# K's seventh block product by quarter products, and three moves around it, in two attention layers on one Trainium2 core

## The chip, the core and the metric

The kernel runs on one core of a Trainium2 chip. Five engines work side by side and meet at semaphores: TensorE (PE in the profile; its weight loads are PEld), VectorE (DVE), ScalarE (ACT), GpSimd (POOL) and SyncE (SP), which issues the DMA transfers. Only TensorE multiplies matrices, and it writes to PSUM; VectorE and ScalarE read PSUM, GpSimd reads only SBUF. Each engine takes its instructions in the order in which the program wrote them. The metric is the device time of one execution in microseconds (us). All arithmetic is in float32.

## What is computed

Two layers of the same form follow one another over x of shape (8, 512, 32, 32): 8 images, 512 channels, 1024 pixels (tokens). Per layer and image:

```python
xn = group_norm(x)                               # layer 0: 8 groups, scale and bias; layer 1: 32 groups
qkv = einsum('oc,bcn->bon', qkv_w, xn) + qkv_b   # 1536 x 512 weights
q, k, v = split(qkv)                             # 8 heads of 64 channels
attn = softmax(einsum('bhdi,bhdj->bhij', q, k) / sqrt(64))
out = einsum('bhij,bhdj->bhdi', attn, v)
x = einsum('oc,bcn->bon', proj_w, out) + proj_b + x
```

## The kernel before

**Units.** One layer of one image is a unit; units 0 to 7 are layer 0, units 8 to 15 are layer 1. Each unit has two stages. In the projection stage TensorE forms Q, K and V of the unit (unit 0: Q, V, K) and then the output projection of the unit before (`project`). In the attention stage it goes through 8 chunks (4 head pairs by 2 halves of the query tokens) of 8 steps: scores (L809), exponential on ScalarE (L817), products with V (L837), row sums on VectorE (L854, L856).

**Block products.** A projection multiplies 512 x 512 weights by 512 x 1024 activations. `blocks` splits both into two by two blocks and needs seven block products instead of eight, at the price of additions. They are numbered 1 to 7 and come in the order 1, 6, 2, 7, 5, 4, 3. The factors are sums and differences of blocks: `mix_weights` makes those of the weights, `mix_right` those of the activations (`t1`, `t2`, `t4`, and in place `b12 = b22 - b12`, the right factor of product 7). Products 1, 2 and 3 accumulate in PSUM over others: `bx`, `by` and `bz` are two banks each (apair[0], sbank[0], apair[1]), and after each product VectorE or ScalarE takes what is finished (`c11`, `summed`, `others`) before a later product writes there. A plain block product (`block_product`, L413) is four matmuls of 128 partitions by 512 columns in Q, K and the projection, eight of 256 columns in V.

**Inner products.** For the block products listed in `INNER` a second level of the same scheme is used in all units but 0 (`inner_products`, L452): the 256 x 256 by 256 x 512 product becomes seven matmuls of 128 x 128 by 256 columns. Their left factors lie ready in DRAM (`mix_inner_left` made them once per layer in three 128 x 128 tiles per block product; `load_inner_left` fetches them for each unit). Their right factors are four subtractions of 128x256 per block product (`mix_inner`), by GpSimd for Q's and by VectorE for K's first (room: K's output tile 3, not yet written). Four of the seven results are not added by TensorE. ScalarE copies them from PSUM to a tile of four quarters (L457) as soon as they stand, since the next of them is accumulated on top of the last (1, then 6, then 7, in the region `one`; 5 in the region `two`). GpSimd adds them later: two folds (L467, L468) and then adds into q, k or the result (`rests`, L635 to L638 and L734).

**What sets the order of the work.** It is written by hand. `rest` maps a number g to a list of small steps; `projections` calls the steps of g when it has passed the g-th of 21 marks, seven in each of its three projections (`done`). `attention` returns the steps that the next unit's projections carry for this unit: `parts`. Mark 3 has the last head pair's reciprocals, mark 10 its division and its bias (`divide_last`: L919 on VectorE, two L926 on ScalarE), 15 the load of the projection's left factors, 17 to 20 the projection's right factors (mixing and `mix_o`, the latter on GpSimd for unit 6, B - 2). A step recorded at a mark stands in its engine's queue at that place. Steps called from the marks show in the profile under L566, whatever they do.

**Norm of the next unit.** While a unit is in attention, `at_step` runs the next unit's group norm: statistics (L277), aggregation (L281), group means and variances by small matmuls with a group matrix (L289), scale and shift (L315 to L327), application on ScalarE (L331) and the first two right factors (L179). In unit 0 all but the statistics come one chunk later than in other units (`late`). At the very start `norm_first` norms unit 0's input in two halves, with idle matmuls between the small ones (L358), which multiply x's first tile with itself; nothing reads their result.

**Rooms.** Tiles come from pools with a fixed number of buffers; a tile's first writer waits until the readers of the one before in that buffer are done. Here: `o1`, `o2`, `o4` of `tpool` (room for Q's copies, then the projection's factors), `p` (4), `acc` (2), `tr` (2, among them u2 of Q, K, V and the projection, and the projection's left factors) and `rb` (1: the last pair's reciprocals, then the projection's u3).

Of the kernel before, what the change touches and what calls it, by code (L numbers as in the profile page):

```python
# [11 lines left out]
F32 = mybir.dt.float32  # L12
# [6 lines left out]
P = 128  # L19
# [13 lines left out]
def fast_path(ctx, tc, x, qkv_wT, proj_wT, vecs, groups, out, flag):  # L33
# [15 lines left out]
    nc = tc.nc  # L49
    B, C, N = x.shape  # L50
    CC = C // P
    D = C // HEADS
    NT = N // P
# [4 lines left out]
    BL = 32  # L58
    SCALE = 1.0 / math.sqrt(D)

    INNER = {"q": (2, 5, 4, 3), "k": (1, 2, 5, 4, 3), "o": (2, 3, 4)}
    assert D == H and C == FD

    def pool(name, bufs, **kw):
# [135 lines left out]
        s1, s2, s4 = made  # L200
        return {1: a11, 2: a12, 3: s4, 4: a22, 5: s1, 6: s2, 7: a21}

    def mix_inner_o(u, right, k, engine):


        sub = engine.tensor_sub
        b = right[k]
        b11, b12 = b[:, 0, :FD2], b[:, 0, FD2:]
        b21, b22 = b[:, 1, :FD2], b[:, 1, FD2:]
        tag = {2: "x2", 3: "x1", 4: "x4"}[k]  # L210
        t = tpool.tile([P, 4, FD2], F32, tag=tag, name=f"ro{k}_{u}")
        t1, t2, t4 = (t[:, i, :] for i in range(3))
        sub(t1, b12, b11)
        sub(t2, b22, t1)
        sub(b12, b22, b12)
        sub(t4, b21, t2)
        return {1: b11, 2: b21, 3: b22, 4: t4, 5: t1, 6: t2, 7: b12}, t[:, 3, :]

    def mix_inner_left(l, lefts):

# [124 lines left out]
    def norm_first(xs, weights, mixing):  # L345

        bank = sbank[1][:, 0, :]  # L350
        (
            (first, stats_1, aggregate_1, means_1, variances_1, scales_1, apply_1, apply_now_1),
            (second, stats_2, aggregate_2, means_2, variances_2, scales_2, apply_2, apply_now_2),
        ) = (norm_parts(0, xs, lo, lo + 2) for lo in (0, 2))

        def idle_products(n):
            for _ in range(n):
                nc.tensor.matmul(  # L358
                    sbank[0][:, 0, : 2 * P], xs[:, 0, :P], xs[:, 0, : 2 * P], start=True, stop=True
                )  # L360

        idle_products(3)
        for h in range(NH):
            stats_1(0, h)
        mixing_w = weights(first["last"])
        for h in range(NH):
            stats_1(1, h)
        aggregate_1()
        stats_2(2, 0)
        means_1(bank)  # L370
        idle_products(3)
        stats_2(2, 1)
        variances_1(bank)
        idle_products(4)
        for h in range(NH):
            stats_2(3, h)
        aggregate_2()
        scales_1()
        apply_now_1(0, 0)
        apply_1(1, 0)  # L380
        apply_now_1(0, 1)
        apply_1(1, 1)
        means_2(bank, first["last"])
        idle_products(3)
        mixing_w[0]()

        def rest():
            variances_2(bank)
            mixing[0]()
            scales_2()  # L390
            for h in (1, 0):
                apply_now_2(2, h)
                apply_2(3, h)
            mixing[1]()
            mixing_w[1]()

        return rest, mixing_w
# [19 lines left out]
                )  # L417

    def blocks(name, left, right, tokens, c11, others, done, u3_in, summed, inner={}, rests=None,
               between=None, behind=None, p1=None):  # L420

# [10 lines left out]
        def inner_products(bank, k, first=False):  # L434
# [25 lines left out]
                step(j)  # L460
            return (rest, partial(step, order[-1])) if k == 1 else rest

        def add_rest(r, h, rest, alone=None):

            if rest is not None:
                add = nc.gpsimd.tensor_add
                add(rest[:, 0, FD2:], rest[:, 0, FD2:], rest[:, 1, FD2:])  # L467
                add(rest[:, 1, FD2:], rest[:, 1, :FD2], rest[:, 1, FD2:])  # L468
                rests(r, h, rest, alone)

        def work(pool, tag, k):
# [18 lines left out]
        else:  # L490
# [4 lines left out]
            nc.scalar.copy(p1, bx)  # L495
            done(sums)
            products(by, 6, True, False)
        u2 = work(trpool, "tr", "u2")
        summed(0, u2, by, p1)
        done(sums)  # L500
        rest = inner_products(bx, 2, fresh)
        c11(bx, p1 if fresh else None, rest)
        add_rest(0, 0, rest)
        done(sums)
        products(by, 7, False, False)
        u3 = work(*u3_in, "u3")
        summed(1, u3, by, p1)
        done(sums)
        twice = inner_products(bz, 5, True)
        others(1, 1, bz, u3, twice)  # L510
        add_rest(1, 1, twice, u3)
        done(sums)
        rest = inner_products(by, 4)
        others(1, 0, by, p1)
        add_rest(1, 0, rest)
        done(sums)
        rest = inner_products(bz, 3)
        others(0, 1, bz, u2, twice)
# [14 lines left out]
    def inner_of(w, sel, left):  # L533


        x, z, s1 = apair[0], apair[1], sbank[1]
        p = room_of(ppool, "p")
        plan = {
            "q": {
                2: (s1, z, ORDER, room_of(tpool, "o1")), 5: (s1, x, ORDER, room_of(tpool, "o2")),  # L540
                4: (x, s1, ORDER, room_of(tpool, "o4")), 3: (s1, x, ORDER, room_of(tpool, "o1")),
            },
            "k": {
                1: (s1, z, ORDER_1, lambda _: w.k[1].rearrange("p (a b) -> p a b", a=2)),
                2: (s1, z, ORDER, room_of(tmppool, "tmp")),
                5: (s1, x, ORDER_5, p), 4: (x, s1, ORDER, p), 3: (s1, x, ORDER, p),
            },
        }[sel]
        return {
            k: (inner_lefts(k, left[k], w.made[sel][k]), w.inner[k], *plan[k]) for k in INNER[sel]  # L550
        }

    def projections(w, rest, between=None):
# [94 lines left out]
        def values():  # L648
            w.v = vpool.tile([P, NT, C], F32, tag="v", name=f"v_{u}")

            def of_tokens(t):
                return t.rearrange("p a (b o) -> p (a b) o", b=2)

            def v11(bank, more, _):
                to, cols = w.v[:, : NT // 2, :FD2], of_tokens(bank)
                w.last["v"].append(
                    nc.scalar.copy(to, cols) if more is None else
                    nc.vector.tensor_add(to, cols, of_tokens(more))
                )

            def v_others(r, h, bank, more, _=None):
                w.last["v"].append(
                    nc.vector.tensor_add(
                        w.v[:, ts(h, NT // 2), ts(r, FD2)], of_tokens(bank), of_tokens(more)
                    )
                )

            blocks(
                f"v_{u}", w.lefts[2], w.right, True, v11, v_others, done, (ppool, "p"), plain_sum,
                **early["v"],  # L670
            )

# [101 lines left out]
    def attention(w, at_step, at_end):  # L774
# [185 lines left out]
        transposed(n_chunks - 1)  # L960
        reduced(n_chunks - 1)

        def divide_last():
            divide(CC - 1)
            for h in range(NH):
                add_bias(CC - 1, h)

        w.right_o, mixing = mix_right(f"o_{u}", *w.ao)
        w.inner_o = None
        parts = {3: [lambda: reciprocals(CC - 1)], 10: [divide_last], 17: mixing[:2], 18: mixing[2:3],  # L970
                 19: mixing[3:]}
        if u in (0, B):
            return parts

# [12 lines left out]
        def mix_o(k):  # L987

            engine = nc.gpsimd if u == B - 2 else nc.vector
            right, room = mix_inner_o(u, w.right_o, k, engine)  # L990
            if k == INNER["o"][-1]:
                lefts.append(room[:, :P])
                nc.sync.dma_start(lefts[-1], src[:, len(lefts) - 1, :])
            w.inner_o[k] = right

        def finish():
            for i, k in enumerate(INNER["o"]):
                w.inner_o[k] = (inner_lefts(k, w.left[k], lefts[3 * i : 3 * i + 3]), w.inner_o[k])

        parts[15] = [load_left]  # L1000
        parts[18] += [partial(mix_o, 2)]
        parts[19] += [partial(mix_o, 3)]
        parts[20] = [partial(mix_o, 4)]
        w.finish = finish
        return parts

# [26 lines left out]
    for u in range(2 * B):  # L1033
# [10 lines left out]
        if u > 0:  # L1044
            w.made, w.inner, parts = old.made_next, {}, {}
            for k in INNER["q"]:
                room = ppool.tile([P, 4, FD2], F32, tag="p", name=f"r{k}_{u}")
                w.inner[k], parts[k] = mix_inner(right[k], room, nc.gpsimd)

            room = w.k[3].rearrange("p (a b) -> p a b", a=4)  # L1050
            w.inner[1], parts[1] = mix_inner(right[1], room, nc.vector)
            for part in parts[2] + parts[5]:
                part()  # L1053
            for g, k in ((2, 4), (3, 3), (5, 1)):
                rest.setdefault(g, []).extend(parts[k])
        if u == B + 1:
            rest.setdefault(16, []).extend(mixing_o)
# [11 lines left out]
        if u == 0:  # L1069
            def first_left_part(i, part):  # L1070
# [1 line left out]


            after = [14] * len(INNER["q"]) + [
                14 + {1: 1, 2: 3, 5: 5, 4: 6, 3: 7}[k] for k in INNER["k"]
            ]
            for i, part in enumerate(mix_inner_left(0, dict(zip("qk", lefts)))):
                rest.setdefault(after[i], []).append(partial(first_left_part, i, part))
# [59 lines left out]
            if old.u == B - 1:  # L1138
                (left_o,), mixing_o = mix_weights(1, [load_proj(1, "wproj")], nc.vector, 3)


        late = 1 if u == 0 else 0

        def at_step(s, state):
            if nxt is None:
                return
            st, stats, aggregate, means, variances, scales, apply, _ = nxt
            c, t = divmod(s, NT)

            if left_parts and t in (3, 7) and s >= (3 + late) * NT - 1:  # L1150
                left_parts.pop(0)(state["exp"][-1])

            pair = (c + 1) % 2
            free = state["free"][pair]
            c -= late
            if u == 0 and NT // 2 <= s < NT:
                stats_of(2 * s - NT, 2 * s - NT + 1)
            if c == 1 and t == 1:
                aggregate()
# [27 lines left out]
        nc.vector.tensor_reduce(low[:, 1:2], okay, AX.X, ALU.min)  # L1187
        nc.vector.tensor_mul(both, low[:, 0:1], low[:, 1:2])

    project_last(old, [part for g in (3, 10) for part in rest[g]] + [verdict])  # L1190
    nc.tensor.matmul(turns[0][:1, :1], both, ones[:, :1], start=True, stop=True)
    nc.scalar.copy(flag, turns[0][:1, :1])

# [262 lines left out]
```

## Time and profile before

| | |
|---|---|
| median of 4 runs | 3269.28 us (3268.52 to 3269.92) |
| profiled execution | 3269.09 us, span 3267.3 us, TensorE clock 1.00 |
| busy in the span | PE 3253.4, DVE 2612.5, ACT 1623.9, POOL 1092.5 us |
| one inner unit's projection stage, unit 2 | 404.61 to 496.27 us, PE busy 91.66 of 91.66 |
| the same stage, others | DVE 63.62, ACT 26.39, POOL 59.64 us busy |
| one attention stage, unit 1 | 294.35 to 404.61 us, PE busy 110.26 of 110.26 |

The profile is of one execution. A row of the timeline is an instruction, or several alike in a row: start in us from the span's start, length, engine, line of the program, operation, tile written and tiles read, shape, count, and in brackets the idle time of that engine before it with what ended it. float32 matmuls leave two records each; their ends are modelled, so distances between starts tell more than lengths. In the list of waits the columns are: who waited for whom, us in total, times, longest.

### The profile page before, as it was taken

The page shows a single profiled execution, that of the slowest core. Times are in us where ns is not written, and L with a number is a line of the kernel's source. Part 1 is how long each engine was busy: PE and PEld are TensorE (multiplying, and loading weights), DVE is VectorE, ACT ScalarE, POOL GpSimd, SP SyncE. Part 2 cuts the span into 40 slices and gives each one's busy share as a digit, 9 for nine tenths or more (in the row PEclk, how much of TensorE's full clock was granted, in tenths as well). Part 3 has the DMA queues.
Part 4 walks back from the last instruction along what each step waited for, and adds up shares of the span by engine and source line. Part 5 has one row for each costly group of instructions (what it writes and reads, how often), then busy time and mean ns, then how long its engine had stood idle before and what let it go on. Part 6 is the DMA issues. An engine that isn't in the chain of part 4 may idle for free.

```text
span 3267.3 us, 56136 instructions
## 1 busy us (share of the span) xinstructions
PE 3253.4 (100%) x22080; PEld 1839.8 (56%) x22080; DVE 2612.5 (80%) x3364; ACT 1623.9 (50%) x2212; POOL 1092.5 (33%) x1125
## 2 busy tenths in 40 slices
PE   9999999999999999999999999999999999999999
PEld 5455474654746547465574645646556474564743
DVE  5886968879687896878968779687896978969777
ACT  1652726536274462744627436373563735637354
POOL 2051161531616216066160603506125061340610
PEclk9999999999999999999999999999999999999999
DMA  2112120121201212023120111201212012120221
GB/s 94 41 43 78 40 83 28 49 79 43 79 28 43 79 44 85 22 69 114 48 85 29 56 61 55 85 15 42 86 43 85 15 45 83 43 85 15 67 74 48
DMA packets 78395, 188.54 MB, mean 58 GB/s; under 512 B 22064, under 2 KB 27056, under 8 KB 78128
## 3 DMA queue, kind: packets, MB, share of 16 engines
q1 hardware_dynamic: 78128, 184.88, 16.4%
q8 instruction: 179, 2.93, 0.4%
q14 instruction: 88, 0.72, 0.1%
HBM read 144.47 MB, written 38.80 MB: 56 GB/s over the span
## 4 chain that ended last, share of the span: by engine, by line
PE 99%; DVE 0%; DMA 0%; ACT 0%; issue 0%; SPq 0%; DVEq 0%; ACTq 0%
PE a L837 27%; PE s L809 26%; PE s L413 16%; PE a L413 13%; PE a L452 9%; PE s L452 7%; PE a L809 1%; PE s L755 0%; PE a L755 0%; DMA xn<-x_dram 0%; PE s L358 0%; DVE stats L277 0%; PE a L289 0%; ACT p L817 0%; DVE u_q L612 0%
## 5 line engine op out<-in xcount | busy, mean ns | idle before, releaser
L817 ACT ACTIVATE p<-s 128x1024 f32<-128x1024 f32 x976 | 998.3, 1024 | 597.5 <-PE s L809 567.2
L837 PE MATMUL a<-p,v 64*64 64x512 f32 x8192 | 1099.7, 589 | 0.2 <-ACT p L817 0.2
L809 PE MATMUL s<-q,k 64*64 64x512 f32 x7808 | 1058.1, 590 | 0.0
L856 DVE TENSOR_TENSOR acc<-acc,p 128x1024 f32<-128x1024 f32 x768 | 964.2, 1255 | 75.5 <-ACT p L817 22.1
L837 PEld LDWEIGHTS a<-p,v 64*64 64x64 f32 x8192 | 382.7, 131 | 496.7 <-ACT p L817 350.9
L809 PEld LDWEIGHTS s<-q,k 64*64 64x64 f32 x7808 | 383.4, 133 | 432.8 <-issue 426.0
L1053 POOL TENSOR_TENSOR r<-xn 128x256 f32<-128x256 f32 x30 | 52.3, 1743 | 1135.6 <-DVE acc L856 807.2
L854 DVE TENSOR_TENSOR acc<-p,p 128x1024 f32<-128x1024 f32 x128 | 156.4, 1222 | 17.5 <-ACT p L817 17.5
L309 POOL TENSOR_TENSOR y<-var,half 128x4 f32<-128x4 f32 (+1 forms) x17 | 33.1, 1949 | 401.1 <-DVE var L307 401.1
L638 POOL TENSOR_TENSOR k<-k,m_k 128x512 f32<-128x512 f32 x120 | 165.8, 1397 | 0.0
L869 DVE STREAM_TRANSPOSE tr<-acc 128x1024 f32<-128x1024 f32 x128 | 158.0, 1234 | 0.0
L879 DVE TENSOR_REDUCE red<-tr 128x32 f32<-128x1024 f32 x128 | 153.9, 1202 | 0.6
L638 POOL TENSOR_TENSOR q<-q,m_q 128x512 f32<-128x512 f32 x120 | 153.1, 1290 | 0.0
L863 DVE TENSOR_TENSOR ao<-a,tmp 128x512 f32<-128x512 f32 x128 | 88.0, 687 | 66.7 <-ACT tmp L862 66.7
L467 POOL TENSOR_TENSOR m_o<-m_o 128x256 f32<-128x256 f32 x39 | 28.7, 736 | 332.9 <-ACT m_o L457 332.9
L495 ACT COPY p_o<-a 128x1024 f32<-128x1024 f32 x15 | 15.2, 1012 | 244.1 <-PE a L413 244.1
L526 DVE TENSOR_TENSOR u_v<-s,p_v 128x1024 f32<-128x1024 f32 x32 | 39.2, 1224 | 121.2 <-POOL k L635 96.2
L457 ACT COPY m_q<-s 128x256 f32<-128x256 f32 x150 | 55.9, 373 | 146.7 <-PE s L452 132.6
L413 PE MATMUL s<-x_t,s2w 128*128 128x512 f32 x256 | 117.5, 592 | 0.0
L413 PE MATMUL s<-xn,w 128*128 128x512 f32 x256 | 115.5, 594 | 1.8 <-DVE xn L179 1.8
L413 PE MATMUL a<-w,xn 128*128 128x256 f32 x496 | 112.1, 379 | 0.0
L926 ACT ACTIVATE ao<-ao,vec 128x512 f32<-128x512 f32 x128 | 88.4, 714 | 43.0 <-DVE ao L919 43.0
(296 smaller groups left out, 4884.1 us busy)
## 6 DMA issues: line engine op xcount, KB each, us to landing
rb<-drec SPq DMA_DIRECT2D x128, 256.0 KB, 3.9
xn<-mid SPq DMA_DIRECT2D x36, 512.0 KB, 7.7
xn<-x_dram SPq DMA_DIRECT2D x32, 512.0 KB, 7.0
x<-x_dram SPq DMA_DIRECT2D x32, 512.0 KB, 4.8
il<-ilk SPq DMA_DIRECT2D x15, 960.0 KB, 6.3
x<-mid SPq DMA_DIRECT2D x28, 512.0 KB, 4.6
il<-ilq SPq DMA_DIRECT2D x15, 768.0 KB, 4.3
mid<-u_o SPq DMA_DIRECT2D x32, 256.0 KB, 2.0
```

The lines of the kernel that those rows point to most:

```text
L413: nc.tensor.matmul(dst, at[:, c, ts(i, P)], moving[:, c, :], start=start and c == 0 and not (tokens and i % 2), stop=stop and c == 1, skip ...
L452: nc.tensor.matmul(dst[j], a[j], b[j], start=j in (1, 5) or first and j in (2, 4), stop=j not in (1, 6), skip_group_check=True,)
L638: w.last[sel].append(add(cols, cols, rest[:, i, :]))
L809: nc.tensor.matmul(bank[e * H : (e + 1) * H, j, :], w.k[pr][j * H : (j + 1) * H, t * P + e * H : t * P + (e + 1) * H], w.q[pr][j * H : (j ...
L817: exp = nc.scalar.activation(p, bank, AF.Exp, scale=SCALE)
L837: nc.tensor.matmul(banks[r][j * H : (j + 1) * H, :], w.v[rows, t, lo : lo + D], p[rows, j, :], start=(t == 0), stop=(t == NT - 1),)
L854: nc.vector.tensor_add(acc, state["first"], p)
L856: nc.vector.tensor_add(acc, acc, p)
L863: i1 = nc.vector.tensor_add(w.ao[pr // 2][:, pr % 2, ts(qh, FD)], banks[1], tmp)
L869: nc.vector.transpose(tr, state["acc"].pop(c))
L879: nc.vector.tensor_reduce(red[:, :, qh, :], state["tr"].rearrange("p j (f i) -> p j f i", i=BL), AX.X, ALU.add)
L926: nc.scalar.activation(cols, cols, AF.Identity, bias=vec[:, units[u][0], VB, pr : pr + 1])
```

## The change

It has four parts.

1. K's product 7 joins the inner products (`INNER["k"]`), in units 1 to 15. Its right factors are made by VectorE at mark 7, in the room of K's output tile 2; its results are copied to the room `o4`. Since product 7's result goes into two outputs, its copies are folded once and added twice (`rests` for (1, 1) and (1, 0)). The left factors in DRAM grow from five to six for K.
2. The bias of the last head pair moves from mark 10 to mark 14, behind K's last copy; the division stays at 10.
3. The projection's later factors (b12, t4, and the inner ones of products 4 and 3) move from marks 18 to 20 to mark 21, behind V's last take. Those of products 2 and 3 are no longer made in place. V's u2 goes to the pool `rb` in units with inner products.
4. `late` is gone: unit 0's norm steps for unit 1 stand in the same chunks as in other units. And all idle matmuls at the start but the first three multiply the group matrix instead of x.

```diff
-    INNER = {"q": (2, 5, 4, 3), "k": (1, 2, 5, 4, 3), "o": (2, 3, 4)}
+    INNER = {"q": (2, 5, 4, 3), "k": (1, 2, 7, 5, 4, 3), "o": (2, 3, 4)}
...
-    def mix_inner_o(u, right, k, engine):
+    def mix_inner_in(b, t, engine):
         sub = engine.tensor_sub
...
-        def idle_products(n):
+        def idle_products(n, of=gmat.rearrange("p l m -> p (l m)")):
             for _ in range(n):
                 nc.tensor.matmul(
-                    sbank[0][:, 0, : 2 * P], xs[:, 0, :P], xs[:, 0, : 2 * P], start=True, stop=True
+                    sbank[0][:, 0, : 2 * P], of[:, :P], of[:, : 2 * P], start=True, stop=True
                 )
-        idle_products(3)
+        idle_products(3, xs[:, 0, :])
...
+        def fold(rest):
+            add = nc.gpsimd.tensor_add
+            add(rest[:, 0, FD2:], rest[:, 0, FD2:], rest[:, 1, FD2:])
+            add(rest[:, 1, FD2:], rest[:, 1, :FD2], rest[:, 1, FD2:])
...
-        u2 = work(trpool, "tr", "u2")
+        u2 = work(*u2_in, "u2")
...
-        products(by, 7, False, False)
+        seventh = inner_products(by, 7)
         u3 = work(*u3_in, "u3")
         summed(1, u3, by, p1)
+        if seventh is not None:
+            fold(seventh)
         done(sums)
         twice = inner_products(bz, 5, True)
         others(1, 1, bz, u3, twice)
         add_rest(1, 1, twice, u3)
+        if seventh is not None:
+            rests(1, 1, seventh)
         done(sums)
         rest = inner_products(by, 4)
         others(1, 0, by, p1)
         add_rest(1, 0, rest)
+        if seventh is not None:
+            rests(1, 0, seventh)
...
-                2: (s1, z, ORDER, room_of(tmppool, "tmp")),
+                2: (s1, z, ORDER, room_of(tmppool, "tmp")), 7: (z, s1, ORDER, room_of(tpool, "o4")),
...
+                u2_in=(rbpool, "rb") if w.inner else (trpool, "tr"),
...
-        def divide_last():
-            divide(CC - 1)
+        def bias_last():
             for h in range(NH):
                 add_bias(CC - 1, h)
...
-        parts = {3: [lambda: reciprocals(CC - 1)], 10: [divide_last], 17: mixing[:2], 18: mixing[2:3],
-                 19: mixing[3:]}
+        parts = {
+            3: [lambda: reciprocals(CC - 1)], 10: [lambda: divide(CC - 1)], 14: [bias_last],
+            17: mixing[:2], 21: [mixing[3], mixing[2]],
+        }
...
-        parts[18] += [partial(mix_o, 2)]
-        parts[19] += [partial(mix_o, 3)]
-        parts[20] = [partial(mix_o, 4)]
+        parts[18] = [partial(mix_o, 2)]
+        parts[21] += [partial(mix_o, 4), partial(mix_o, 3)]
...
-            room = w.k[3].rearrange("p (a b) -> p a b", a=4)
-            w.inner[1], parts[1] = mix_inner(right[1], room, nc.vector)
+            for k, pr in ((1, 3), (7, 2)):
+                room = w.k[pr].rearrange("p (a b) -> p a b", a=4)
+                w.inner[k], parts[k] = mix_inner(right[k], room, nc.vector)
             for part in parts[2] + parts[5]:
                 part()
-            for g, k in ((2, 4), (3, 3), (5, 1)):
+            for g, k in ((2, 4), (3, 3), (5, 1), (7, 7)):
...
-                14 + {1: 1, 2: 3, 5: 5, 4: 6, 3: 7}[k] for k in INNER["k"]
+                14 + {1: 1, 2: 3, 7: 4, 5: 5, 4: 6, 3: 7}[k] for k in INNER["k"]
...
-        late = 1 if u == 0 else 0
...
-            c -= late
...
-    project_last(old, [part for g in (3, 10) for part in rest[g]] + [verdict])
+    project_last(old, [part for g in (3, 10, 14) for part in rest[g]] + [verdict])
```

## The prediction

> **What bounds the kernel now.** I read the chain of work that ended last first, then TensorE's waits, then the timeline of unit 2 (its projections run from 404.61 to 496.27 us) engine by engine, and last the two places outside it that the change touches. The chain by engine (the page's part 4), then all that TensorE waited for:
>
> ```profile
> PE 99%; DVE 0%; DMA 0%; ACT 0%; issue 0%; SPq 0%; DVEq 0%; ACTq 0%
> ```
> ```profile
> PE s L358 <- DMA xn<-x_dram: 4.4, 1, 4.4
> PE s L413 <- DVE xn L179: 1.8, 1, 1.8
> PE s L358 <- DVE xn L338: 0.9, 1, 0.9
> ```
>
> TensorE is the path from start to end, and only single waits are left on it. So time goes in two ways: less TensorE work, or one of those waits. Everything else in the change is free until it makes TensorE late. K's seventh product in unit 2, TensorE's timeline (start, length, engine, line):
>
> ```profile
> 433.69 0.59 PE L452 MATMUL s<-xn,w 128*128 128x256 f32 x2
> 434.12 0.59 PE L452 MATMUL a<-xn,w 128*128 128x256 f32 x2
> ...
> 436.28 0.59 PE L452 MATMUL s<-r,w 128*128 128x256 f32 x2
> 436.71 3.60 PE L413 MATMUL s<-xn,w 128*128 128x512 f32 x8
> 440.14 0.59 PE L452 MATMUL s<-x_t,s1w 128*128 128x256 f32 x2
> ```
>
> Each matmul leaves two records, and the next product starts before the last record's drawn end, so starts are what to read. The seventh product as four matmuls of 128x512 takes 440.14 - 436.71 = 3.43 us; the second, as seven of 128x256, takes 436.71 - 433.69 = 3.02.
>
> **Part 1: K's seventh by quarters, 15 units.** TensorE: 15 x (3.43 - 3.02) = 6.2 us less. Of the page "TensorE: Matmul & The Clock Gate", section "Back-to-back issue gap", one rule speaks against it: at 128 columns it gives about 81 ns sustained against 56 by its formula, because weight loads fill the gap. An estimate from that, 25 ns on each of 14 records, would cost 0.35 of the 0.41 us and leave 0.9 us in all. This trace contradicts it: 0.43 us per 128x256 matmul is half of 0.86 per 128x512, the loads hidden.
>
> What can take it back is the copying. The quarters' first result must be copied by ScalarE before the fourth matmul adds onto it. ScalarE there:
>
> ```profile
> 436.91 0.37 ACT L457 COPY m_k<-s 128x256 f32<-128x256 f32 x1 [0.49 <-PE s L452]
> 437.18 0.51 ACT L604 ACTIVATE k<-p_k,vec 128x256 f32<-128x256 f32 x1
> 439.00 1.33 ACT L926 ACTIVATE ao<-ao,vec 128x512 f32<-128x512 f32 x2 [1.32 <-DVE ao L919]
> ```
>
> The bias of L926 waits for the division and would have blocked the new copies; it moves behind K, where ScalarE idles 3.12 us before p_v's copy. Its reader, the projection's first factor, comes 6 us later. L604 stays in front of the new copy: it ends at 437.69, the copy overlaps its end by 0.10 as the neighbours do, and ends at 437.59 + 0.37 = 437.96. The fourth matmul is due at 436.71 + 3 x 0.43 = 438.00. What does being that close cost? Unit 2 has a case, a factor of GpSimd that is 0.02 us late:
>
> ```profile
> 425.81 0.59 PE L452 MATMUL a<-r,il 128*128 128x256 f32 x2
> 426.26 0.70 PE L452 MATMUL a<-r,s4w 128*128 128x256 f32 x2
> 426.80 0.59 PE L452 MATMUL s<-r,s4w 128*128 128x256 f32 x2
> ```
>
> From 425.81 to 426.80 should be 0.86 and is 0.99: 0.02 late costs 0.13, since the weight load isn't early any more. With 0.05 from an end to its listener (VectorE ends at 211.35 in unit 1, TensorE goes at 211.40) the copy is 0.01 late: 0.11 to 0.12 per unit, 1.7 us in 15. Bounds: nothing, and 0.18 (2.7 us) if the listener takes 0.11, as a weight load at 412.75 after a copy ending at 412.63. I take 1.7, the nearest row. Net of part 1: -4.5.
>
> VectorE gets four subtractions (room: k's third tile) between Q's last take and K's first sums:
>
> ```profile
> 421.77 1.26 DVE L566 TENSOR_TENSOR k<-xn 128x256 f32<-128x256 f32 x1
> 423.06 0.83 DVE L566 TENSOR_TENSOR k<-xn,k 128x256 f32<-128x256 f32 x1
> 423.82 0.94 DVE L566 TENSOR_TENSOR k<-xn 128x256 f32<-128x256 f32 x1
> 424.68 0.94 DVE L566 TENSOR_TENSOR k<-xn,k 128x256 f32<-128x256 f32 x1
> ...
> 427.00 1.02 DVE L624 TENSOR_TENSOR q<-a,u_q 128x512 f32<-128x512 f32 x2
> 430.43 0.83 DVE L486 TENSOR_TENSOR k<-k 128x256 f32<-128x256 f32 x1 [2.40 <-ACT k L457]
> ...
> 432.58 0.42 DVE L488 TENSOR_TENSOR p_k<-a,k 128x256 f32<-128x256 f32 x1 [0.49 <-ACT k L457]
> ```
>
> Like the four of L566, each will end about 0.28 after an instruction of GpSimd ends: 1.26 beside a 128x512 add, 0.87 apart beside 128x256 ones. GpSimd has one 128x512 (to 428.93) and then short ones, so they run from 427.95 to 431.82. That fills the 2.40 us in which VectorE now waits for ScalarE and pushes what follows: L486 ends at 432.69 instead of 431.26, L487 at 433.51, L488 at 433.85. The matmul at 434.12 overwrites what L487 and L488 read; its weight load wants them by about 433.96. Spare: 0.11 us. Cost 0; lower bound 0 (nothing waits now); upper bound four times 1.26, 1.2 us later, 15 x 1.2 = 18 us.
>
> GpSimd gets two folds (0.73 each) and four adds of 128x512 (1.25) per unit, 6.4 us. It now ends K's sums at 461.49; with the added work and longer turns beside VectorE I get 470.4. Room o4 is Q's until about 435.3, needed at 437.6. Attention needs k at 495. V's u2 waited for GpSimd (7.39 idle on VectorE) and now sits in rb, free since the division at 438.97. GpSimd's longer run slows VectorE's factors in V: four subtractions of the second product from 464.07 to 468.07, then V's fifth take to 469.2. V's third product writes that bank from 469.6. Spare: about 0.3. Cost 0; the upper bound is under the rivals. Factors 4 and 3 now come behind V's last take (473.2 to 479.7); the sixth's take comes at 480.2 and the projection's seventh product, first user, at 483. The factors of unit 6 are GpSimd's, behind K's sums; I get 487 at the latest in unit 2's clock, for use at 490. SP's projection weights still wait for V's fourth product, not for these, and the loads of x behind them on SP's queue stand where they stood. The weight load of K (1.15 MB for 0.96) lands some 0.5 us later, at 412, needed at 427; the row sums' transfers queued behind it have slack. Four more instructions and one store per layer make the factors of K's weights, behind the product that last reads them.
>
> **Part 2: unit 0's norm a chunk sooner.** VectorE's factors of x_1 leave the last chunk, so unit 1's Q needn't wait:
>
> ```profile
> 211.40 3.70 PE L413 MATMUL s<-xn,w 128*128 128x512 f32 x8 [1.76 <-DVE xn L179]
> ```
>
> That product should have begun at 209.48: -1.9, and the 0.1 of a late start. Bounds: unit 2, where the factors lie a chunk from the end, waits 0; units 8 and 12 wait 0.3. Attention of unit 0 takes 110.65 against 110.26 in others: a step of 1.26 for 0.86 at 137.98, in the chunk where scales and reciprocals meet: -0.4. Against it, the statistics of x_1 end only at 105.6, and VectorE is 1.1 us behind unit 1's pace:
>
> ```profile
> 107.24 1.19 DVE L854 TENSOR_TENSOR acc<-p,p 128x1024 f32<-128x1024 f32 x1
> ```
>
> The aggregation (0.42) would end at 108.77, and the mean's matmul is due at 88.83 + 19.79 = 108.62 (unit 1's place): 0.3 late. Then the reduction, two additions (2.54) and four small steps (0.75) end at 112.98 against 112.47: 0.7. So +1.0. Net -1.4 (-2.4 to -0.4).
>
> **Part 3: idle matmuls on the group matrix.** The last three waited for a normalised half that they needn't read:
>
> ```profile
> 14.69 1.56 PE L358 MATMUL s<-xn 128*128 128x256 f32 x6 [0.94 <-DVE xn L338]
> 16.09 1.88 PE L413 MATMUL a<-xn,w 128*128 128x512 f32 x4
> ```
>
> They can follow the mean's matmuls at 13.8 and end at 15.07; the first real product has its halves at 14.85. 16.09 - 15.07 = -1.0 (-1.2 to 0, if weights bind; they land by 18.2, and the third is used at 22.3).
>
> **Sum.** -4.5 - 1.4 - 1.0 = -6.9 on the profiled execution's 3269.09 (span 3267.3 and 1.8 around it). The median of runs, 3269.28, is 0.2 above: 3262.3.
>
> **Rivals.** That the change doesn't do what it says is excluded for the order of work: the built program has seven matmuls of 128x256 where four of 128x512 stood, in each of 15 units.
> *The covers hold fully* (no late copy, no late mean): -6.2 - 2.4 - 1.0 = -9.6, 3259.7. For it: no inner product's copy in Q or K delays TensorE today. Against: L604 stands in no other product's way.
> *The partial sums in V collide.* If one more of the four subtractions meets a 128x512 add, 0.54 later, V's third product waits 0.3 and starts 0.1 slow: 0.4 x 12 units = 4.9, so 3267.2, no change that counts.
> *Slower: VectorE's new factors.* All four meet long adds: K's second product waits 1.2 per unit, 3262.3 + 18 = 3280. It decides from 0.47 us of wait per unit (6.9 / 15). Against: GpSimd's order there is fixed, one long add and then short ones.
>
> **How the numbers follow.** Likeliest, 0.58: 3262.3, its own range 3260.8 to 3264.2. Covers hold 0.14; V collides 0.20; slower 0.08. Range: from 3259.5 to 3267.3, which leaves out the slower one and some ends. 0.2% is 6.5 us, about what a measurement of this kernel can tell from no change: 3262.7 and 3275.8. The likeliest straddles 3262.7, six parts in ten below: 0.35, and 0.14 make faster 0.49; slower 0.08; same the remaining 0.43.
>
> **What would show it.** Right: K's seventh as fourteen records of 128x256 in 3.02 to 3.15 us, with a gap of 0.1 at the fourth matmul; VectorE's four k subtractions ending near 431.8 in unit 2's place and no wait at K's second product; unit 1's Q without its 1.76; matmul L289 of unit 0 late by 0.3 and 0.7; the first real product near 15.1. Wrong: TensorE waiting on VectorE in K or V in every unit, or on GpSimd's room o4.

## The result

The changed kernel takes 3274.38 us (median of 37 runs), the kernel before 3269.13 (57 runs): a ratio of 1.0017, 95% interval 1.0012 to 1.0022. It is 5.25 us slower, where 6.9 us less was forecast. The profiled execution took 3275.41, its span 3273.6.

First all that TensorE waits for in the changed kernel (engine, line, engine waited for; us in total, times, longest):

```profile
PE a L448 <- ACT m_o L453: 7.9, 1, 7.9
PE s L354 <- DMA xn<-x_dram: 4.3, 1, 4.3
PE s L409 <- DVE u_v L531: 1.3, 1, 1.3
PE a L285 <- DVE e L298: 1.2, 2, 0.8
PE s L285 <- DMA gmat<-groups_dram: 1.0, 1, 1.0
```

The 1.8 of unit 1's Q and the 0.9 of the idle matmuls are gone; a wait of 7.9 on a copy of ScalarE and one of 1.3 on VectorE are new. Both are found stage by stage. Busy time of each engine (and number of instructions) by stage, with TensorE's granted clock: the projections of units 1, 2, 7 and 9, before:

```profile
199.49:294.35 94.86, 93.10 (x338) 62.98 (x334) 60.96 (x78) 22.17 (x48) 54.88 (x56) 1.00 0.24 86
404.61:496.27 91.66, 91.66 (x354) 66.38 (x352) 63.62 (x90) 26.39 (x59) 59.64 (x63) 1.00 0.25 90
1414.12:1505.79 91.67, 91.67 (x354) 66.50 (x353) 67.86 (x86) 26.40 (x59) 81.09 (x91) 1.00 0.34 121
1818.63:1911.54 92.91, 92.91 (x337) 63.12 (x335) 62.58 (x81) 22.30 (x48) 52.52 (x55) 1.00 0.26 88
```

and after:

```profile
199.52:292.30 92.78, 92.73 (x343) 64.14 (x341) 62.24 (x81) 23.57 (x52) 60.62 (x61) 1.00 0.25 90
402.56:493.82 91.26, 91.26 (x360) 67.43 (x358) 70.10 (x94) 27.66 (x63) 68.41 (x69) 1.00 0.25 92
1410.72:1513.13 102.41, 94.45 (x361) 69.24 (x359) 70.94 (x90) 27.67 (x63) 88.66 (x98) 0.95 0.31 112
1826.20:1920.29 94.09, 92.78 (x343) 64.09 (x341) 68.47 (x85) 23.57 (x52) 62.34 (x61) 1.00 0.25 89
```

The columns after the stage are its length, PE, PEld, DVE, ACT, POOL, then clock, DMA share and GB/s. Unit 1 gains 2.1; unit 7 loses 10.7, at a mean clock of 0.95; unit 9 loses 1.2; all others gain 0.2 to 0.5. GpSimd has 88.66 us of work in unit 7's stage, more than in any other of these. The rest of the difference of the spans (6.3): the start 0.55 less, attention of units 0 and 7 each 0.6 more, where a small matmul of the norm waits for VectorE (0.44 and 0.76, the fourth line above), and attention of unit 2 0.25 more.

What holds unit 7? TensorE's timeline there, then ScalarE's:

```profile
1496.70 0.59 PE L448 MATMUL s<-o_t,wproj_wproj 128*128 128x256 f32 x2
1497.13 0.59 PE L448 MATMUL s<-o_t,ro 128*128 128x256 f32 x2
1505.63 1.22 PE L448 MATMUL a<-ro,lo 128*128 128x256 f32 x2 [7.91 <-ACT m_o L453]
1506.64 1.06 PE L448 MATMUL s<-ro,lo 128*128 128x256 f32 x2
...
1511.31 0.59 PE L448 MATMUL s<-ro,lo 128*128 128x256 f32 x2
```
```profile
1489.28 0.37 ACT L453 COPY m_o<-s 128x256 f32<-128x256 f32 x1 [0.49 <-PE s L448]
1505.21 0.37 ACT L453 COPY m_o<-a 128x256 f32<-128x256 f32 x1 [15.56 <-POOL x L740]
```

The copy waits for GpSimd. In the kernel before, the same copy waited for TensorE alone:

```profile
1500.36 0.37 ACT L457 COPY m_o<-a 128x256 f32<-128x256 f32 x1 [7.00 <-PE a L452]
```

The copies of the projection's fourth product go into the room of its second. That room is free when GpSimd has folded the second's rest (L461, L462) and added it (L740). GpSimd's queue up to there:

```profile
1475.75 0.73 POOL L1007 TENSOR_TENSOR ro<-ao 128x256 f32<-128x256 f32 x1
...
1484.25 1.04 POOL L209 TENSOR_TENSOR ro<-o_t 128x256 f32<-128x256 f32 x1 [4.70 <-DVE o_t L179]
...
1492.39 0.46 POOL L225 TENSOR_TENSOR lw<-w 128x128 f32<-128x128 f32 x1
...
1500.81 0.45 POOL L231 TENSOR_TENSOR lw<-s4w,lw 128x128 f32<-128x128 f32 x1
1501.22 0.72 POOL L461 TENSOR_TENSOR m_o<-m_o 128x256 f32<-128x256 f32 x1
1502.01 0.72 POOL L462 TENSOR_TENSOR m_o<-m_o 128x256 f32<-128x256 f32 x1
1502.69 2.48 POOL L740 TENSOR_TENSOR x<-x,m_o 128x512 f32<-128x512 f32 x2
```

K's sums to 1475.79, unit 6's factors (to 1492.44) with a pause of 4.70 for a half-product of VectorE that now comes later, then sixteen small operations (the factors of four of layer 1's left matrices, issued by unit 7's projection at its first step), and only then the fold. Before, the same sixteen operations stood in the same place. But K's sums ended at 1471.00, the pause was 1.71, and the additions began at 1496.16 and took 2.49:

```profile
1467.52 3.48 POOL L638 TENSOR_TENSOR k<-k,m_k 128x512 f32<-128x512 f32 x2
...
1475.18 0.73 POOL L215 TENSOR_TENSOR ao<-ao 128x256 f32<-128x256 f32 x1 [1.71 <-DVE o_t L179]
...
1496.16 2.49 POOL L734 TENSOR_TENSOR x<-x,m_o 128x512 f32<-128x512 f32 x2
```

They ended at 1498.65, 1.7 us ahead of the copy at 1500.36. Now they end at 1505.17. Counted from the start of the stage that is 9.9 us later: K's sums end 8.2 later, the pause is 3.0 longer, the sixteen operations take 1.3 less. The spare of 1.7 us is read nowhere in the prediction.

Unit 9's wait is in V, on VectorE (L571 makes the projection's left factors of layer 1, in this unit alone):

```profile
1878.73 0.87 DVE L571 TENSOR_TENSOR s1w<-wproj_wproj 128x512 f32<-128x512 f32 x1
...
1884.55 1.74 DVE L179 TENSOR_TENSOR o_t<-ao 128x1024 f32<-128x1024 f32 x1
1887.88 1.21 DVE L531 TENSOR_TENSOR u_v<-s,p_v 128x1024 f32<-128x1024 f32 x1
```

The four of L571 and two of L179 run from 1878.73 to 1887.95, 9.2 us, five of them at 1.6 to 1.8 us beside GpSimd's longer K sums; before, the same six took 7.5. The sum of L531 behind them is late, and TensorE starts its product 1.47 us behind its pace. In the kernel of experiment 2 that has K's seventh whole and keeps the moves, unit 9's stage is 92.91 and this wait is absent: K's seventh brings it.

### The profile page after: what moved, and what is told of

It reads as the page before. It is cut to its first block, busy times and chain, and to the rows that moved or that the text cites. A ratio compares the mean times of both kernels' runs of the same rounds, so it can differ in the third digit from the quotient of the medians.

```text
span 3273.6 us, 56587 instructions
## 1 busy us (share of the span) xinstructions
PE 3251.8 (99%) x22170; PEld 1869.2 (57%) x22170; DVE 2694.1 (82%) x3424; ACT 1643.5 (50%) x2272; POOL 1225.0 (37%) x1223
## 5 line engine op out<-in xcount | busy, mean ns | idle before, releaser
L862 DVE TENSOR_TENSOR acc<-acc,p 128x1024 f32<-128x1024 f32 x768 | 963.4, 1254 | 74.4 <-ACT p L823 21.7
L815 PEld LDWEIGHTS s<-q,k 64*64 64x64 f32 x7808 | 390.9, 133 | 425.4 <-issue 418.0
L643 POOL TENSOR_TENSOR k<-k,m_k 128x512 f32<-128x512 f32 x180 | 258.7, 1458 | 0.0
L531 DVE TENSOR_TENSOR u_v<-s,p_v 128x1024 f32<-128x1024 f32 x32 | 39.2, 1225 | 128.2 <-PE s L409 128.2
L461 POOL TENSOR_TENSOR m_o<-m_o 128x256 f32<-128x256 f32 x39 | 28.7, 735 | 221.6 <-ACT m_o L453 221.6
L453 ACT COPY m_k<-s 128x256 f32<-128x256 f32 x165 | 61.5, 373 | 93.8 <-PE s L448 90.2
L327 ACT ACTIVATE xn<-xn,shift,scale 128x512 f32<-128x512 f32 x124 | 99.5, 804 | 12.6 <-DVE shift L323 12.6
```

Of the source, the lines that this page charges most:

```text
L327: nc.scalar.activation(cols, cols, AF.Identity, bias=st["shift"][:, c - lo : c - lo + 1], scale=st["scale"][:, c - lo : c - lo + 1],)
L453: taken.append(nc.scalar.copy(to[j], dst[j]))
L643: w.last[sel].append(add(cols, cols, rest[:, i, :]))
L815: nc.tensor.matmul(bank[e * H : (e + 1) * H, j, :], w.k[pr][j * H : (j + 1) * H, t * P + e * H : t * P + (e + 1) * H], w.q[pr][j * H : (j ...
L862: nc.vector.tensor_add(acc, acc, p)
```

## The experiments

Twelve kernels ran, each between runs of the kernel before on the same chip; "before" below is the median of those.

**1. The sixteen operations out of the way** (their first step to the seventh):

```diff
-                    for part in {1: made_parts[:4], 7: made_parts[4:]}.get(g, ()):
+                    for part in {7: made_parts}.get(g, ()):
```

> Only edit to the changed kernel: the first four of layer 1's ten left-factor parts (16 operations of GpSimd in unit 7's projection, 1492.39 to 1501.26 us) move from the projection's first step to its seventh. Theory Q (GpSimd's queue in unit 7 makes the fold late that frees ScalarE's copy): the first fold starts about 8.8 us sooner, at 1492.4, the two additions behind it end at 1496.4 instead of 1505.17, the copy is due about 1497.5; the wait of 8.07 goes, and with it the ten matmuls of 128x256 at 0.427 instead of 0.216 behind it (2.3 us): 3274.4 - 10.4 = 3264.0 (3263.5 to 3265, as the parts run longer into attention of unit 7). Rival C (the granted clock of 0.998 is a property of the denser TensorE work all along): above 3270. Rival F (TensorE waits for the moved factors themselves): the wait stays at 8, 3274.

Measured 3270.46 (before 3268.82). The wait in unit 7's projection is gone: the stage is 92.30, at a clock of 1.00. So GpSimd's queue held it. But 5.6 of the 10.1 us gained in the stage come back in attention of unit 7, which takes 116.81 instead of 111.24. The operations stand now in front of the next norm's step on GpSimd:

```profile
1537.62 0.46 POOL L231 TENSOR_TENSOR lw<-s4w,lw 128x128 f32<-128x128 f32 x1
1538.04 1.02 POOL L305 TENSOR_TENSOR y<-var,half 128x4 f32<-128x4 f32 x1
```
```profile
DVE y L311 <- POOL y L305: 5.2, 1, 5.2
```

VectorE waits 5.2 us for it, its row sums stop, ScalarE's exponentials wait for those, and TensorE pauses 4.06. My expectation looked past the queue a second time.

**2. Which part fills the queue?** One kernel undoes the move of unit 6's factors, one undoes K's seventh, one has neither.

```diff
         parts[18] = [partial(mix_o, 2)]
-        parts[21] += [partial(mix_o, 4), partial(mix_o, 3)]
+        if u == B - 2:
+            parts[18] = [mixing[2], partial(mix_o, 2)]
+            parts[19] = [mixing[3], partial(mix_o, 3)]
+            parts[20] = [partial(mix_o, 4)]
+            parts[21] = []
+        else:
+            parts[21] += [partial(mix_o, 4), partial(mix_o, 3)]
```

> The changed kernel with unit 6's projection factors and the half-products of ao (mixing 2 and 3) at the steps 18, 19, 20 of before; all other units as changed. If the move of the last half-product to step 21 holds GpSimd (its 4.70 us of waiting for VectorE's L179 in unit 6's factors), GpSimd's queue ends 4.7 sooner, the wait of 8.07 becomes 3.4, 3269.7 (3269 to 3271). If the move is innocent and K's seventh alone fills GpSimd's queue: wait 8, 3274.4. If VectorE's half-products then meet V's takes in unit 7, up to 2 more.

```diff
-    INNER = {"q": (2, 5, 4, 3), "k": (1, 2, 7, 5, 4, 3), "o": (2, 3, 4)}
+    INNER = {"q": (2, 5, 4, 3), "k": (1, 2, 5, 4, 3), "o": (2, 3, 4)}
...
-            for k, pr in ((1, 3), (7, 2)):
+            for k, pr in ((1, 3),):
```

> The changed kernel with K's seventh as four whole matmuls again; the moves, the norm and the idle matmuls stay. TensorE gets 15 x (0.41 - 0.10) = 4.6 us more. If the moved half-product holds GpSimd in unit 7, GpSimd only waits longer for it (11 for 4.7) and the wait of TensorE stays near 8: 3274.4 + 4.6 - 1.2 (unit 9's wait) = 3277.8 (3276.5 to 3279). If the two folds and four additions of K's seventh are what makes GpSimd late (6.4 of the 8.07 us): wait 1.7, no slow matmuls behind it: 3269 (3268 to 3271).

The third is the kernel before with parts 2 and 3 of the change alone:

```diff
-        late = 1 if u == 0 else 0
...
-            c -= late
...
-        def idle_products(n):
+        def idle_products(n, of=gmat.rearrange("p l m -> p (l m)")):
...
-        idle_products(3)
+        idle_products(3, xs[:, 0, :])
```

> The kernel before with parts 2 and 3 alone (unit 0's norm a chunk sooner, idle matmuls on the group matrix). From the two profiles: unit 1's Q -1.8, attention of unit 0 +0.6 (the mean 0.3 late, the variance 0.7, the 0.4 at 137.98 gone), start -0.55 to -1.0: 3269.1 - 2.0 = 3267.1 (3266.6 to 3267.6). If the gain of unit 1's Q needs part 1: 3269.

Measured: old order 3272.86, seventh whole 3276.18, neither 3266.05 (before 3268.82). TensorE's wait in unit 7, from the starts of its matmuls: 6.64 with K's seventh and the old order, 7.39 with the move and no seventh, 8.07 with both, none with neither. Either edit alone is enough. All three medians lie outside the ranges given: the first 1.9 above, the others 0.3 and 0.6 below. With the seventh whole, GpSimd is done with K's sums 7 us sooner and then waits for the moved half-product:

```profile
1483.54 1.04 POOL L209 TENSOR_TENSOR ro<-o_t 128x256 f32<-128x256 f32 x1 [12.08 <-DVE o_t L179]
```

That theory stands, with a wait of 7.4 for 8. The one for the old order is right in direction and wrong in size, 1.4 less for 4.7. The pause of 4.70 goes, but VectorE's half-products now run beside GpSimd. K's sums there end at 1476.04 in a unit that began 1.85 earlier, so 2.1 later than in the changed kernel, and more of the factors take 1.17 for 0.73:

```profile
1479.40 1.17 POOL L1007 TENSOR_TENSOR ro<-ao,ro 128x256 f32<-128x256 f32 x1
1480.53 0.73 POOL L1007 TENSOR_TENSOR ro<-ao 128x256 f32<-128x256 f32 x1
```

The kernel with neither gained 2.8 (ratio 0.9993, interval 0.9984 to 1.0002, so not shown by the median alone). Its profile has unit 1's projection at 92.84 for 94.87, attention of unit 0 at 111.24 for 110.65: part 2 doesn't need part 1.

**3. Spreading the left factors over the attention** (into other rooms, not shown in the cut), and two further waits on top of that.

```diff
-                if u == B - 1:
-                    for part in {1: made_parts[:4], 7: made_parts[4:]}.get(g, ()):
-                        part()
...
                     lambda _, i=i: [part() for part in mixing_w[i : i + 2]] for i in (0, 2)
-                ]
+                ] + [
+                    lambda step, i=i: [part(step) for part in made_parts[i : i + 2]]
+                    for i in range(0, len(made_parts), 2)
+                ]
```

> The changed kernel; all ten left-factor parts of layer 1 leave unit 7's projection and are spread over its attention, two every half chunk from the fourth chunk on, behind the norm's step on GpSimd (L305). Theory Q (GpSimd's queue, nothing else): neither the 8.07 us of the changed kernel nor the two waits that the move to the seventh step brought (4.06 and 1.01 in attention of unit 7, 0.69 before it): 3270.5 - 0.9 - 6.6 = 3263.0 (3262.5 to 3263.8). If two parts at a time slow VectorE's row sums: up to 3265. If something else than the queue held unit 7: above 3268.

Measured 3267.46 (before 3268.24): 4.5 above what I expected. Unit 7's projection is 92.28, but its attention 114.52. The theory on the queue isn't touched, the price of the cure was wrong: as I read the trace, two GpSimd parts at a time cost VectorE's row sums more than the second branch allowed.

```profile
1566.01 4.10 DVE L862 TENSOR_TENSOR acc<-acc,p 128x1024 f32<-128x1024 f32 x3
1570.57 4.27 DVE L862 TENSOR_TENSOR acc<-acc,p 128x1024 f32<-128x1024 f32 x3 [0.46 <-DVE acc L862]
```

These take 1.37 and 1.42 each, where the mean of L862 in the changed kernel is 1.254. In attention, where VectorE is busy 102.77 of 111.24 us (unit 7 of the changed kernel), that is not hidden. That it makes up the whole 4.5 us is not shown. A wait of 0.69 before the first score stayed, partly on ScalarE's copies; I did not follow it.

Beside unit 7 there is a small cost in every unit. In the changed kernel the fourth matmul of K's seventh product adds onto a result that ScalarE copies only just in time, and its second record starts 0.104 late (its lines stand under "What held"). The next kernel also puts K's bias (L609 of the changed kernel, L604 before) behind the copies of the seventh's quarters (`c11` hands that one instruction back as `tail`):

```diff
-        c11(bx, p1 if fresh else None, rest)
-        add_rest(0, 0, rest)
+        tail = c11(bx, p1 if fresh else None, rest)
+        if tail is None:
+            add_rest(0, 0, rest)
         done(sums)
         seventh = inner_products(by, 7)
+        if tail is not None:
+            tail()
+            add_rest(0, 0, rest)
```

> As the kernel with the parts spread, and in K the bias of L598 behind the copies of the seventh's quarters instead of ahead of them. If it is ScalarE's late copy that costs 0.104 us at the fourth quarter of every seventh product: 15 x 0.104 = 1.6 less, 3261.4 (3261.1 to 3261.9), and each projection 91.26 instead of 91.36. If the 0.104 is the price of a change of bank or operand: 3263.0.

Measured 3267.81, no gain, projections of 91.36 still: by my two branches, "the price of a change of bank". The trace says otherwise. The 0.104 has left the seventh product; the bias at 438.40 now delays the fifth's copy, and the 0.104 is there:

```profile
438.40 0.51 ACT L614 ACTIVATE k<-p_k,vec 128x256 f32<-128x256 f32 x1
438.81 0.36 ACT L453 COPY m_k<-s 128x256 f32<-128x256 f32 x1
```
```profile
439.22 0.70 PE L448 MATMUL s<-r,il 128*128 128x256 f32 x2
439.76 0.59 PE L448 MATMUL a<-x_t,il 128*128 128x256 f32 x2
```

The third of this group adds two edits:

```diff
+        if u == B:
+            parts[17], parts[19] = mixing[:1], mixing[1:2]
...
+            if u == 0:
+                c, t = divmod(s - 2, NT)
```

> As the kernel with the copy first, and two more edits: unit 8's second half-product of ao at step 19 instead of 17 (unit 9's wait of 1.43 in V), and unit 0's norm steps two steps (1.7 us) later (the mean's 0.305 and the variance's 0.722 in attention of unit 0). If both waits are of VectorE being late by those amounts: 3261.4 - 1.4 - 1.0 = 3259.0 (3258.5 to 3259.8). If the half-product makes V's next take late instead, or unit 1's first product waits again for its factors: 3260 to 3262.

Measured 3266.39. The first edit works: unit 9's stage falls from 94.09 to 92.53. The second doesn't: attention of unit 0 stays at 111.25. The mean now meets other work of VectorE and is late, which puts TensorE 0.46 behind; the rest of the 1.0 comes in steps of 0.12 to 0.17 in the chunks after it, and why is not shown. Unit 1's projection is 93.30 for 92.79: its Q waits 0.2 for a factor and 0.4 for a sum, both VectorE's.

Part 3 of the change also ran alone:

> The kernel before with part 3 alone (the last 15 idle matmuls on the group matrix). By the step of the prediction 1.0 less than before; by the kernel with parts 2 and 3 (2.8 less, of which 2.0 in unit 1's Q, and 0.6 and 0.4 given back in attention of units 0 and 7) 1.7 less. So 1.0 to 1.7 less: 3267.1 to 3267.8. If weights or the group matrix bind: 3268.8.

That kernel, the one before with the idle matmuls of part 3 alone, took 3266.95 against 3268.24, 1.3 less (ratio 0.9996, interval 0.9987 to 1.0005).

**4. Unit 7 as before.** The seventh whole in unit 7, and unit 6's factors at their old steps as in experiment 2:

```diff
-            for k, pr in ((1, 3), (7, 2)):
+            for k, pr in ((1, 3), (7, 2))[: 1 if u == B - 1 else 2]:
```

In this and the next two kernels unit 7's seventh product uses a left matrix of which one quarter already holds a factor's difference, so unit 7's K is not the reference's; the work is the same.

> The changed kernel, with unit 7's seventh product of K whole and unit 6's factors and half-products at their old steps (so GpSimd's queue in unit 7 holds what it held before); the other 14 units as changed. Theory Q: no wait in unit 7, its projection 91.67 as before and its attention 110.6 to 111.1: 3274.4 - 10.7 - 0.3 = 3263.4 (3262.6 to 3264.0). If K's seventh in units 1 to 6 already carries a delay into unit 7: 3266 or more.

Measured 3263.81 (before 3268.59): unit 7's projection 91.67, its attention 110.98, as the theory had it. On it, the bias between the first and the second copy of the seventh's quarters, and unit 8's half-product at step 19:

```diff
...
                     taken.append(nc.scalar.copy(to[j], dst[j]))
+                    if j == 1 and behind_first is not None:
+                        behind_first()
...
```

> As the kernel with unit 7 as before, and two edits more: in K the bias of L598 between the first and the second copy of the seventh's quarters, and unit 8's second half-product of ao at step 19. If the late copy is what costs 0.104 per seventh product: 14 x 0.104 = 1.5 less, projections of 91.26; unit 9's wait of 1.43 gone: 1.5 less; 3260.4 (3259.8 to 3261.2). If the place of the bias only moves the delay to the next product's copy (as with the bias behind all copies): 3261.9.

Measured 3260.43. The seventh product runs without the 0.104, and ordinary projections take 91.26:

```profile
434.22 0.59 PE L448 MATMUL s<-xn,il 128*128 128x256 f32 x2
434.65 0.59 PE L448 MATMUL a<-k,il 128*128 128x256 f32 x2
435.08 0.59 PE L448 MATMUL s<-k,il 128*128 128x256 f32 x2
```

So the late copy is the cause of the 0.104: it moved with the bias in experiment 3 and is gone when the copies stand clear of it.

On top of that kernel, a fourth idle matmul at the start:

```diff
-        idle_products(3, xs[:, 0, :])
+        idle_products(4, xs[:, 0, :])
```

> As the kernel before this one, with a fourth idle matmul on x at the start, so that TensorE doesn't pause before the first mean. In the ten profiles so far the matmuls took 0.427 until 8.5 to 9.9 us where TensorE's pause at 7.3 was 0.16 or less, and until 12.3 to 13.9 where it was 0.27 or more, and the first attention began at 86.2 to 86.8 or at 88.2 to 88.8. If the pause restarts the slow clock: matmuls at full speed by 9.9, the first attention at 86.2 to 86.8, the median 0 to 1.5 less than the kernel before this one, 3259.5, and its runs closer together. If the pause is an effect and not the cause: either start, no change.

Measured 3261.29: no gain. TensorE didn't pause at 7.3 and yet reached full speed at 10.5, the first attention at 87.40; the kernel without the fourth had 11.1 and 87.17 with a pause of 0.19, and the kernel with unit 7 as before 11.1 and 87.15 with one of 0.13. So the pause alone doesn't decide the start.

The last kernel gives unit 7's K its right factor back:

> The kernel with unit 7 as before, the bias between the copies and unit 8's half-product at step 19, with one more 128x128 subtraction of GpSimd ahead of unit 7, which puts back the quarter of the left factor that layer 0's factors replaced (the three kernels before this one take unit 7's seventh product of K with that quarter replaced, so unit 7's K is not the reference's; the work is the same). One operation of 0.46 us in attention of unit 6, where GpSimd is idle for tens of us: 3260.4 as without it (3259.8 to 3261.3). If that subtraction delays unit 7's factors: up to 0.5 more.

```diff
+            if u == B - 1:
+                a21 = lefts[1][7][:, 0, P:]
+                nc.gpsimd.tensor_sub(a21, lefts[1][7][:, 0, :P], a21)
```

Measured 3260.54 (before 3268.57): ratio 0.9977, interval 0.9968 to 0.9986, faster than the kernel before, and so than the changed one. The projections of units 7 and 9 (stage, its length, then the engines as above):

```profile
1407.94:1499.60 91.66, 91.66 (x354) 66.50 (x352) 67.45 (x86) 26.26 (x59) 82.37 (x92) 1.00 0.34 123
1812.37:1904.79 92.42, 92.42 (x343) 64.20 (x341) 68.57 (x85) 23.66 (x52) 62.33 (x61) 1.00 0.25 90
```

GpSimd has 82.37 us of work in unit 7's stage, near the 81.09 of before, and nobody waits for it there.

## Why the prediction was wrong

**The step that failed.** "The factors of unit 6 are GpSimd's, behind K's sums; I get 487 at the latest in unit 2's clock, for use at 490." The number held: they end at 1492.44, and less 1410.72 - 404.61 that is 486.3. What failed is the question. I asked when the factors are used, not what GpSimd has to do behind them: sixteen operations and the fold that frees ScalarE's room. The spare of that queue was 1.7 us in the trace of before, and its work came 9.9 us later. Cost 0 was 8.07 of waiting, and the additions alone or the moved factors alone would have brought 6.64 or 7.39 (experiment 2). With 2.65 of slow matmuls behind it and 0.32 ahead of it, for another sum of VectorE, unit 7's stage was 11.05 over the 91.36 of an undisturbed one. The signs of being wrong that the prediction lists, room o4 among them, didn't show: TensorE waited at a room of the output projection. In the other units but 9 the same additions were free, as forecast.

**A rival that came elsewhere.** "V collides" was priced at 0.4 over the 12 units whose V queue on VectorE holds the subtractions of the projection's second product. In none of them does TensorE wait in V. The same collision of VectorE with GpSimd came in unit 9, which is not among the 12, with 1.47, because V's queue there holds four left factors that my walk through unit 2 didn't contain. Both mistakes are one: unit 2 stood for all fifteen, and units 7 and 9, near the change of layer, have work that no other has.

**Sum.** -6.9 + 11.05 (unit 7) + 1.5 (unit 9: 1.18 more instead of 0.3 less) = +5.65; the medians say +5.25, the two profiled spans +6.3. Not forecast either were the attention of units 2 and 7 (0.25 and 0.6 more), a later factor of GpSimd in unit 1's Q (0.25, not followed), and a start that gave 0.55 for 1.0. (The forecast's own terms end at 3262.4, not 3262.3.)

**What held.** K's seventh: -0.41 and a late copy of 0.11 to 0.12 per unit, so -0.30; measured 0.104 at the fourth matmul in all fifteen units, and stages of 91.36 for 91.67 in the undisturbed ones. In unit 2:

```profile
435.43 0.59 PE L448 MATMUL s<-xn,il 128*128 128x256 f32 x2
435.86 0.70 PE L448 MATMUL a<-k,il 128*128 128x256 f32 x2
436.40 0.59 PE L448 MATMUL s<-k,il 128*128 128x256 f32 x2
```

VectorE's new factors end at 429.67, in a unit that begins 2.05 sooner: 431.72 for my 431.82, with no wait at K's second product. GpSimd's sums of K end at 468.26, so 470.31 for my 470.4. Rival three (VectorE's factors) didn't come. Part 2: unit 1's Q gave 2.0 as forecast; the mean puts TensorE 0.30 behind and the variance 0.66 more, for 0.3 and 0.7; attention of unit 0 is 0.6 longer, for -0.4 + 1.0.

The 25 ns per record that the prediction weighs come from a figure for 128 columns. No matmul here has 128: at 256 columns the records start 0.216 us apart, half of the 0.429 at 512, so the trace shows no loss at 256 and doesn't contradict the figure.

Part 3: the first real matmul started at 15.54 in this execution, not 15.1. The group matrix landed late here (TensorE's 1.0 above), but that is not all: with the same first instructions it started at 13.71 in the kernel with the left factors later, and at 15.80 in the one that is spread with the copy first, which didn't wait for the matrix. Alone the edit measured 1.3 for 1.0, within what the start varies by.

## What to carry to other kernels

A cover is not proved when the moved work is done before its own reader: walk on down that engine's queue to whatever frees a room or a bank for somebody else, and read the spare there in the trace of before. A repeated stage has its exceptions at the seams (first unit, last unit of a layer, the one after), and one of them can cost more than all the others gain, so take one timeline of each kind. Work moved out of one queue's narrow place goes into another's: two of three cures for unit 7 moved the wait into its attention.

## What the hardware did that I had not expected

After the wait of 7.91 us TensorE ran at half speed: the matmuls of 128x256 started 0.427 apart instead of 0.216 from 1505.63 to 1510.5, which cost 2.65 us beside the wait itself (the sum of the excess over 0.216), and the stage's granted clock is 0.95. By the profile's clock it was 1.00 until 1500.5, 0.50 from 1500.6 to 1510.8, and 1.00 again behind: it fell 3 us into the wait and came back 5.2 us after TensorE's next matmul. The waits of 6.64 and 7.39 in experiment 2 were followed by the same distance of 0.427. The wait of 4.06 in attention of unit 7 (experiment 1) left the clock at 1.00. The Trainium skill, page "TensorE: Matmul & The Clock Gate", section "Part 1: The HAM clock gate (the "warmup" mystery)", names this: an idle window of about 3.4 us halves the clock, a busy one of about 3.4 us restores it. An estimate from that page is 1.7 us lost; here it was 2.65. The wait of 4.06 is longer than the page's 3.4 us and didn't halve the clock; here the measurement decides.

At the start, kernels with the same first instructions reached full speed at quite different times, by the distance between their matmuls (the clock column reads 1.00 there even where they start 0.427 apart): 8.7 us (left factors later), 11.1 (unit 7 as before), 12.8 (the changed kernel), 13.9 (spread, copy first). Their first attentions began at 86.56, 87.15, 88.28 and 88.54. So some 2 us of a single execution seem to be no property of the kernel, and a gain at the start is to be read from medians. The same section says that the window runs free, with some 0.5 us of variation; the spread here is 5.2 us, and I have no cause for it.
